# Graph attention on one core: one-hots turned by a compare instead of a transpose, and queries spread in fp32

## The chip, the cores and the metric

The kernel runs on one core of a Trainium2 chip. The metric is the device time of one execution in microseconds. TensorE (PE) multiplies matrices, VectorE (DVE) and ScalarE (ACT) do elementwise work, GpSimd (POOL) issues the gathers, SyncE (SP) issues most other DMAs.

## The reference, cut to what matters

Four pairs of a graph layer and a mixture of experts run one after the other over 3125 nodes with 256 features and 53125 edges, each on the normalized x and added to x. Only the first pair is touched: attention over the edges that end in a node, with 8 heads and the edges' 8 attributes as bias, and then a small mixture of four experts. Up to the order of the additions, the attention is

```python
q, k, v = ln(x) @ Wq.T, ln(x) @ Wk.T, ln(x) @ Wv.T      # 8 heads of 32
logit[e] = scale * (q[dst[e]] * k[src[e]]).sum(-1) + edge_attr_8[e]
a = softmax of logit over the edges with the same dst
x = x + (segment_sum(a * v[src], dst)) @ Wo.T
x = x + experts0(ln(x))      # shared MLP of three layers + 4 experts, the best two weighted
```

The graph, expert and attention layers that follow are the same in both kernels.

## The kernel before, in words

The edges are sorted by destination. The 3125 destinations form T = 25 tiles of P = 125. Each tile has a window of WC = 18 chunks of 128 edges that holds all edges ending in it; edges of a neighbouring tile in that window give one-hot rows of zeros.

**Setup** (lines 1640 to 1787) loads x group by group, normalizes it, writes keys and values to DRAM (kv_d, 2 KB a node in fp32) and the normalized rows, transposed, to lt_d. It fetches the windows' source and destination indices and attributes with indirect DMAs (90 partitions of 128 edges, five times), transposes them so that an edge lies on a partition (turned, L1730), and keeps src_w and row_w (the destination within its tile, bf16). The pools of the setup are then closed.

**The loop** (L1915 to L1950) takes the tiles in three phases at once: now (logits), before (the tile ahead of it: weights, sum, output), after (the next: its one-hots and queries). For one tile these are

- gathered (L1655): 6 indirect DMAs for 6 chunks of keys and values into one of 7 buffers kv, three buffers a tile.
- one_hot (L1797): oh, edges on partitions, 128 x 18 x 126 in bf16, by one comparison (one_hots, L282); also the loads of lt_t (L1804) and eb_t (L1806).
- one_hot_turned (L1821): oht, destinations on partitions: 18 transposes on PE (L1826) and three copies from PSUM on ACT (L1827).
- queries (L1809): q of the tile by one fp32 product of two terms, scaled by ACT (L1815) and split in three bf16 parts whose sum is q: DVE L1816, DVE L1817, ACT L1818, DVE L1819.
- logits (L1831): for every chunk, three bf16 products of oht with the parts of q (L1840) give each edge its query in PSUM (qx, two buffers of two chunks). DVE multiplies the keys with it (L1843) and adds up by head (L1844).
- sums_of (L1848): bias, exponential, sum by destination with oh (L1856).
- weights_of (L1860): the sums' logarithm back at the edges with oht (L1868), subtraction, exponential (L1873).
- weighted (L1875): DVE multiplies the values with the weights (L1878, once for 6 chunks), ACT turns oh into fp32 (oh_f, L1883), PE sums the rows of each destination in fp32 (acc, L1885, 18 products of 265 columns).
- normed, normed_turned, projected (L1889 to L1909): division, transposition, product with Wo, addition to x. normed also keeps deg, the number of a node's edges (L1890).

Between these, beside() runs a step of the experts (Experts0, L793) for two finished tiles at a time: normalize, transposed (L245), gates, and nine hidden products whose bias and ReLU relu_into (L776) gives in turn to DVE (L779) and ACT (L781). Windows prepares indices for the stage after the loop, blocks(), which counts edges between tiles.

The order of the work on each engine is not that of the source: a scheduler that knows the dependences lays the instructions of all engines out, and each engine runs its own list in order. Pools set which buffer an instruction waits for.

```python
pool = tiles          # 2 buffers of each name, opened ahead of the setup
psum = ...            # name="sm" 3 banks, "qx" 2, "acc" 1
```

Of the kernel before, what the change touches and what calls it, by code (L numbers as in the profile page):

```python
# [70 lines left out]
def gnn_ffn_kernel(ctx: ExitStack, tc: tile.TileContext, a, out: bass.AP):  # L71
# [173 lines left out]
    def transposed(psum, dst, src, n, relu=False):  # L245

        for k in range(2):
            ps = psum.tile([128, 512], F32, name="tr")
            for i in range(n):
                nc.tensor.transpose(ps[:, i * P:(i + 1) * P], src[:, i, k * 128:(k + 1) * 128],  # L250
                                    ident[:P, :P])
            of = ps[:, :n * P].rearrange("f (i p) -> f i p", i=n)
            if not relu:
                evacuate(dst[:, k, :n, :], of)
# [518 lines left out]
            evacuate(wt[:ne, :n, :].rearrange("e i p -> e (i p)"), ps[:ne, :n * P])  # L773
            return wt

    def relu_into(dst, ps, bias):  # L776
# [16 lines left out]
    class Experts0:  # L793


        def __init__(self, pools):
            pool = pools.enter_context(tc.tile_pool(name="ex0_b", bufs=1, side="right", reuse_waits="tile"))
            psum = pools.enter_context(tc.tile_pool(name="ps_ex0_b", bufs=1, space=PSUM, side="right",
                                                    reuse_waits="tile"))
            wpool = pools.enter_context(tc.tile_pool(name="w0", bufs=1, side="right", reuse_waits="tile"))  # L800
            with weights_of_pool(wpool, (SLOT0, D)):
                self.group = experts0_by(pool, psum, 2)
            self.now, self.left = iter(()), [(t0, min(2, T - t0)) for t0 in range(0, T, 2)]

        def step(self, ready):
# [5 lines left out]
                return self.step(ready)  # L811
            return False

    def experts0_by(pool, psum, most):

        wp = Packer()
        sw1 = wp.put(kk(a["sW1"]), 128, (2, 256))
# [28 lines left out]
        def group(t0, n):  # L846
# [4 lines left out]
            transposed(psum, lt, ln, n)  # L851
            yield
            g = gates(pool, psum, lt, n, gw, gb, 4, "softmax", ahead)
            yield
# [3 lines left out]
            def hidden(name, m, terms, bias):  # L858
                ps = tr()
                product(ps[:m, :c], terms)  # L860
                relu_into(name, ps[:m, :c], bias)
# [11 lines left out]
            for p in range(2):  # L873
                ps2 = psum.tile([128, 512], F32, name="pair", bufs=1)
                for j in range(2):
                    e = 2 * p + j
                    e1 = pool.tile([128, most * P], F32, name="e1")
                    hidden(e1[:, :c], 128, [(ew1[:, e, k, :], fan(lt[:, k, :n, :])) for k in range(2)],
                           cols[:, 3 + e:4 + e])
                    yield  # L880
                    product(ps2[j * 64:(j + 1) * 64, :c], [(ew2[:, e, :], e1[:, :c])])
                relu_into(e2[:, p, :c], ps2[:, :c], cols2[:, p:p + 1])
# [744 lines left out]
    def attention(windows, experts):  # L1627
# [5 lines left out]
        lt_d = dram.tile([2, 128, T, P], F32, name="lt_d")  # L1633
        eb_d = dram.tile([128, T, H, WC], F32, name="eb_d")
        win_d = dram.tile([T * WC], I32, name="win_d")
        KO, VO, AO = 16, 16 + D, 7
        WB = T * WC // 5
        with ExitStack() as es:
# [96 lines left out]
            def edges_in():  # L1735
# [51 lines left out]
            setup.close()  # L1787


            pool = tiles  # L1790
            psum = es.enter_context(tc.tile_pool(name="ps_att", bufs=3, space=PSUM, reuse_waits="tile"))
            windows.begin(first, lambda: psum.tile([128, 512], F32, name="sm"))

            class Tile:
                pass

            def one_hot(t):  # L1797
                s = Tile()
                s.t, s.kv = t, begun if t == 0 else []
                oh = pool.tile([128, WC, HC], BF16, name="oh")  # L1800
                one_hots(oh, row_h[:, t * WC:(t + 1) * WC, :], iota_h)
                s.oh = oh[:, :, :P]
# [4 lines left out]
                return s  # L1807

            def queries(s):  # L1809
# [8 lines left out]
                nc.scalar.copy(s.q[:, 1, :], q)  # L1818
                nc.vector.tensor_sub(s.q[:, 2, :], q, s.q[:, 1, :])  # L1819

            def one_hot_turned(s):  # L1821
                s.oht = pool.tile([P, WC, 128], BF16, name="oht")
                for c0 in range(0, WC, PC):
                    ps = psum.tile([128, 1024], BF16, name="sm")
                    for c in range(PC):
                        nc.tensor.transpose(ps[:P, c * 128:(c + 1) * 128], s.oh[:, c0 + c, :], ident_h)  # L1826
                    nc.scalar.copy(s.oht[:, c0:c0 + PC, :].rearrange("d c e -> d (c e)"),  # L1827
                                   ps[:P, :PC * 128])
                s.l = pool.tile([128, WC, H], F32, name="l")

            def logits(s, p):  # L1831

                if p == len(s.kv):
                    s.kv.append(gathered(s.t * WC + p * PC))
                kv = s.kv[p]
                for c0 in range(0, PC, 2):
                    ps = psum.tile([128, 2, D], F32, name="qx", bufs=2)
                    for c in range(2):
                        for k in range(3):
                            nc.tensor.matmul(ps[:, c, :], s.oht[:, p * PC + c0 + c, :], s.q[:, k, :],  # L1840
                                             start=(k == 0), stop=(k == 2))
                    k_ = kv[:, c0:c0 + 2, KO:VO]
                    nc.vector.tensor_mul(k_, k_, ps)  # L1843
                nc.vector.tensor_reduce(  # L1844
                    s.l[:, p * PC:(p + 1) * PC, :],
                    kv[:, :, KO:VO].rearrange("p c (h d) -> p c h d", h=H), AX.X, ALU.add)
# [40 lines left out]


            def normed(s):  # L1889
                nc.vector.tensor_copy(deg[:, s.t:s.t + 1], s.acc[:, H:H + 1])  # L1890
                inv = pool.tile([P, H], F32, name="inv")
                nc.vector.tensor_scalar(inv, s.acc[:, 0:H], 1.0e-30, None, ALU.max)
                nc.vector.reciprocal(inv, inv)
                s.ao = pool.tile([P, D], F32, name="ao")
# [4 lines left out]
            def normed_turned(s):  # L1899
                ps = psum.tile([128, 2, P], F32, name="sm")  # L1900
                for k in range(2):
                    nc.tensor.transpose(ps[:, k, :], s.ao[:, k * 128:(k + 1) * 128], ident[:P, :P])
                s.at = pool.tile([128, 2, P], F32, name="at")
                nc.scalar.copy(s.at, ps)

            def projected(s):
# [4 lines left out]
            now, before = one_hot(0), None  # L1911
            one_hot_turned(now)
            queries(now)
            more = experts()
            for t in range(T + 1):  # L1915
                def beside():
                    more.step(t - 1)

                if now:
                    logits(now, 0)  # L1920
                beside()
# [2 lines left out]
                    beside()  # L1924
                    weighted(before)
                beside()
                after = one_hot(t + 1) if t + 1 < T else None
                if before:
                    normed(before)
                if after:  # L1930
# [588 lines left out]
```

## Time and profile before

| What | Value |
|---|---|
| median of 3 runs | 3410.41 us (3407.14 to 3412.61) |
| the profiled execution, its own time | 3415.6 us |
| its span in the profile | 3413.8 us |
| busy PE, DVE, ACT, POOL | 3132.9, 1742.2, 1034.0, 680.0 us |
| attention loop, PE's first turned one-hot to the start of the next stage | about 113 to 925 us |
| start of acc (L1885), first tile and last | 150.9 and 906.2 us |
| mean clock of PE that the throttle granted | 0.951 |

The profile is one execution. A row of a group of instructions has the line, the engine, the operation, the tiles written and read, the shape and the count; then busy us and mean ns of one; then the engine's idle time just before them and what ended it. PE's rows overlap[...]; so the distance of their starts, not their length, is what one costs in a stream. A row of the timeline has the start, the length, the engine, the line and how many instructions were merged in it. PE's weight loads (PEld) run beside its matmuls.

### The profile page before, as it was taken

The numbers are of one execution on the slowest core, as the hardware profiler recorded it, in microseconds if no ns is written. First come the engines' busy times: TensorE is split into PE (matmuls) and PEld (weight loads), VectorE is DVE, ScalarE is ACT, GpSimd is POOL, SyncE is SP. The second block draws the span as 40 slices with busy tenths as digits, with TensorE's granted clock in tenths as the row PEclk, the third lists the DMA queues.
The fourth block names the chain that finished last, engine by engine and source line by source line (L and its number), as shares of the span: only waits on it lengthen the run. The fifth ranks groups of instructions, "written<-read, shape, count | busy, mean of one in ns | idle before, by whom it ended". The sixth has DMA issues, their size and how long they took to land. (4 is left out here: it accounts for less than half of the span.)

```text
span 3413.8 us, 45380 instructions
## 1 busy us (share of the span) xinstructions
PE 3132.9 (92%) x16587; PEld 2446.2 (72%) x16587; DVE 1742.2 (51%) x4905; ACT 1034.0 (30%) x1996; POOL 680.0 (20%) x639
## 2 busy tenths in 40 slices
PE   6688998998888899999996999979999999999898
PEld 2466776777677789898885888868755555579666
DVE  6577778777697534344674122155521111355662
ACT  1222332332255423232331222234423232332120
POOL 1665564655100000000134333200000000000000
PEclk9789998999889999999997999989999999999997
DMA  5755554555256734444344666553200000043001
GB/s 165 235 172 150 160 163 143 160 165 144 61 165 215 192 99 119 102 108 110 91 123 133 185 178 180 167 137 103 69 19 10 10 19 10 7 122 100 21 1 39
DMA packets 253208, 388.23 MB, mean 114 GB/s; under 512 B 41454, under 2 KB 201069, under 8 KB 252973
## 3 DMA queue, kind: packets, MB, share of 16 engines
q1 hardware_dynamic: 184090, 226.68, 23.3%
q0 software_dynamic: 54064, 141.25, 15.3%
q10 hardware_dynamic: 14819, 17.27, 1.9%
q8 instruction: 134, 2.20, 0.3%
q14 instruction: 101, 0.83, 0.1%
HBM read 314.47 MB, written 70.58 MB: 113 GB/s over the span
## 5 line engine op out<-in xcount | busy, mean ns | idle before, releaser
L2222 PE MATMUL agg<-cnt_f,hp 125*128 125x500 f32 (+1 forms) x3500 | 733.1, 369 | 22.2 <-ACT hp L2163 22.0
L2222 PEld LDWEIGHTS agg<-cnt_f,hp 125*128 125x128 f32 x3500 | 635.5, 189 | 103.2 <-ACT hp L2163 23.1
L1660 POOL DMA_INDIRECT kv<-kv_d,src_w x450 | 450.9, 1002 | 281.5 <-PE acc L1885 140.5
L2200 ACT CAST cnt_f<-blk 125x500 fp32r<-125x500 bf16 (+1 forms) x435 | 245.5, 565 | 518.4 <-PE agg L2222 496.7
L2200 DVE CAST cnt_f<-blk 125x500 fp32r<-125x500 bf16 (+1 forms) x440 | 185.5, 423 | 265.5 <-PE agg L2222 221.6
L1382 DVE SCALAR_TENSOR_TENSOR x<-po,gall,x 125x256 f32<-125x256 f32 x200 | 93.8, 484 | 417.5 <-PE po L266 416.9
L1376 ACT ACTIVATE h<-hid_ps,shift,scale 128x500 f32<-128x500 f32 (+1 forms) x224 | 161.9, 723 | 376.0 <-PE hid_ps L266 375.5
L1840 PE MATMUL qx<-q_t,oht 125*128 125x256 bf16 x1350 | 216.2, 296 | 53.9 <-DVE kv L1843 41.2
L1885 PE MATMUL acc<-kv,oh_f 128*125 128x265 f32 x900 | 224.9, 412 | 14.6 <-DVE kv L1878 14.6
L1885 PEld LDWEIGHTS acc<-kv,oh_f 128*125 128x125 f32 x900 | 178.5, 201 | 54.2 <-DVE kv L1878 18.5
L1840 PEld LDWEIGHTS <-oht 125*128 125x128 bf16 x1350 | 138.2, 105 | 100.4 <-issue 50.6
L266 PE MATMUL po<-wslot,h 128*125 128x256 f32 x800 | 203.0, 386 | 0.1
L266 PEld LDWEIGHTS po<-wslot,h 128*125 128x125 f32 x800 | 145.0, 187 | 75.2 <-ACT h L1376 27.0
L266 PE MATMUL hid_ps<-h,wslot 128*128 128x500 f32 (+1 forms) x448 | 193.8, 556 | 4.1 <-ACT h L1376 0.6
L266 PE MATMUL hid_ps<-xe,wslot 128*128 128x256 f32 x832 | 187.3, 383 | 1.8 <-DVE xe L1214 1.8
L1072 POOL DMA_INDIRECT xs_d<-r_l,pos x50 | 60.2, 1204 | 645.3 <-DVE r_l L1068 567.1
L266 PE MATMUL hid_ps<-v_rows,wslot 128*128 128x500 f32 (+1 forms) x448 | 186.8, 537 | 0.0
L1225 ACT ACTIVATE hid<-hid_ps,wslot 128x256 f32<-128x256 f32 x208 | 98.5, 475 | 286.8 <-PE hid_ps L266 286.8
L266 PE MATMUL po<-wslot,hid 128*128 128x256 f32 x832 | 184.5, 378 | 0.0
L266 PEld LDWEIGHTS hid_ps<-xe,wslot 128*128 128x128 f32 x832 | 150.7, 191 | 33.4 <-ACT hid L1225 4.1
L266 PEld LDWEIGHTS po<-wslot,hid 128*128 128x128 f32 x832 | 155.7, 189 | 21.8
L1843 DVE TENSOR_TENSOR kv<-kv,qx 128x512 f32<-128x512 f32 x225 | 150.7, 679 | 26.2 <-PE qx L1840 24.7
(512 smaller groups left out, 4625.8 us busy)
## 6 DMA issues: line engine op xcount, KB each, us to landing
wslot<-in_ex_W SPq DMA_DIRECT2D x52, 1024.0 KB
blk<-an_d SPq DMA_DIRECT2D x60, 546.9 KB
blk<-at_d SPq DMA_DIRECT2D x40, 546.9 KB
blk<-an_d SPq DMA_DIRECT2D x45, 410.2 KB
at_d<-ab SPq DMA_DIRECT2D x25, 683.6 KB
an_d<-an SPq DMA_DIRECT2D x25, 683.6 KB
blk<-at_d SPq DMA_DIRECT2D x30, 410.2 KB
kv<-kv_d,src_w POOLq DMA_INDIRECT x450, 3.7
```

The source lines that it names most:

```text
L266: nc.tensor.matmul(ps, l, r, start=(bias is None and i == 0), stop=(i == last))
L1072: st = nc.gpsimd.indirect_dma_start(out=xs_d, in_=l2[:, i, :].bitcast(I32), in_offset=None, out_offset=bass.IndirectOffsetOnAxis(ap=self.p ...
L1225: nc.scalar.activation(hid[:, m, :], ps[:, :BLK], AF.Gelu, bias=c[:, 4 + m:5 + m])
L1376: nc.scalar.activation(dst[:, m, :c], ps[:, :c], AF.Relu, bias=shift[:, l, col:col + 1], scale=scale[:, l, col:col + 1])
L1382: nc.vector.scalar_tensor_tensor(x[:, t0 + i, :], po, gating.all[:, t0 + i, e:e + 1], x[:, t0 + i, :], ALU.mult, ALU.add)
L1660: got = nc.gpsimd.indirect_dma_start(out=kv[:, c, KO:], out_offset=None, in_=kv_d, in_offset=bass.IndirectOffsetOnAxis(ap=src_i[:, at + c: ...
L1840: nc.tensor.matmul(ps[:, c, :], s.oht[:, p * PC + c0 + c, :], s.q[:, k, :], start=(k == 0), stop=(k == 2))
L1843: nc.vector.tensor_mul(k_, k_, ps)
L1885: nc.tensor.matmul(s.acc[:, :D + H + 1], of[:, c, :], kv[:, c, AO:VO], start=(p == 0 and c == 0), stop=(p == 2 and c == PC - 1))
L2200: to(f[:, :n, :], part[0][:, :n, m % MB, :])
L2222: nc.tensor.matmul(ps[f][:, :c], hp[:, m, k, f * 128:(f + 1) * 128], got[:, :c], start=(m == 0 and k == 0), stop=(m == T - 1 and k == 1))
```

## The change

- **one_hot_turned** no longer transposes. In the setup, the destinations within the tile are also written, in bf16, to a new tensor turned_d in DRAM, 450 chunks of 128 edges. asked(t), at the head of a loop pass, loads the 18 chunks of a tile to all 125 partitions (576 KB), with lt_t and eb_t. DVE compares the loaded rows in place with the partition's number; ACT makes three fp32 copies oht_f of 6 chunks each, in three buffers.
- **queries** ends with ACT's scaling; q stays in fp32. **logits** takes one fp32 product a chunk in place of three bf16 ones.
- **The experts beside the loop** have all their ReLUs and both copies of transposed on ACT. normed copies deg on ACT.
- The loop's tiles lie in a pool of their own, opened after the setup is closed; ao and at have one buffer instead of two.

```diff
@@ relu_into (experts0_by and Experts0 pass on_act=True; transposed gets to=nc.scalar.copy) @@
-        if turn[0]:
+        if turn[0] and not on_act:
             nc.vector.tensor_scalar(dst, ps, bias, 0.0, ALU.add, ALU.max)
         else:
             nc.scalar.activation(dst, ps, AF.Relu, bias=bias)
@@ attention, setup @@
+        turned_d = dram.tile([T * WC, 128], BF16, name="turned_d")
...
+            first_row = pool.tile([WB, 1], F32, name="first_row", bufs=1)
+            nc.vector.memset(first_row, 0.0)
+            for k in range(1, 5):
+                nc.vector.scalar_tensor_tensor(first_row, pcol[:WB], k * WC - 0.5, first_row, ALU.is_gt, ALU.add)
+            nc.vector.tensor_scalar(first_row, first_row, float(P), None, ALU.mult)
...
                         nc.vector.tensor_copy(wf, w)
+                        if to is dst_f:
+                            wr = pool.tile([WB, 128], BF16, name="wr")
+                            nc.vector.tensor_scalar(wr, wf, first_row, float(b * 5 * P), ALU.subtract, ALU.subtract)
+                            nc.sync.dma_start(turned_d[b * WB:(b + 1) * WB, :], wr)
@@ attention, loop @@
-            pool = tiles
+            pool = es.enter_context(tc.tile_pool(name="att_s", bufs=2, reuse_waits="tile"))
...
-            def one_hot(t):
+            def asked(t):
...
+                s.oht = pool.tile([P, WC, 128], BF16, name="oht")
+                move(nc.sync, s.oht.rearrange("d c e -> d (c e)"), turned_d[t * WC:(t + 1) * WC, :].rearrange("(o c) e -> o (c e)", o=1)
+                     .to_broadcast([P, WC * 128]))
                 s.lt = pool.tile([128, 2, P], F32, name="lt_t")
...
-                s.q = pool.tile([P, 3, D], BF16, name="q_t")
-                q = pool.tile([P, D], F32, name="q")
-                nc.scalar.activation(q, ps, AF.Copy, scale=float(HD) ** 0.5)
-                nc.vector.tensor_copy(s.q[:, 0, :], q)
-                nc.vector.tensor_sub(q, q, s.q[:, 0, :])
-                nc.scalar.copy(s.q[:, 1, :], q)
-                nc.vector.tensor_sub(s.q[:, 2, :], q, s.q[:, 1, :])
+                s.q = pool.tile([P, D], F32, name="q")
+                nc.scalar.activation(s.q, ps, AF.Copy, scale=float(HD) ** 0.5)
 
             def one_hot_turned(s):
-                s.oht = pool.tile([P, WC, 128], BF16, name="oht")
+                v = s.oht.rearrange("d c e -> d (c e)")
+                nc.vector.tensor_scalar(v, v, pcol[:P], None, ALU.is_equal)
+                s.oht_f = []
                 for c0 in range(0, WC, PC):
-                    ps = psum.tile([128, 1024], BF16, name="sm")
-                    for c in range(PC):
-                        nc.tensor.transpose(ps[:P, c * 128:(c + 1) * 128], s.oh[:, c0 + c, :], ident_h)
-                    nc.scalar.copy(s.oht[:, c0:c0 + PC, :].rearrange("d c e -> d (c e)"),
-                                   ps[:P, :PC * 128])
+                    s.oht_f.append(pool.tile([P, PC, 128], F32, name="oht_f", bufs=3))
+                    nc.scalar.copy(s.oht_f[-1], s.oht[:, c0:c0 + PC, :])
...
                     for c in range(2):
-                        for k in range(3):
-                            nc.tensor.matmul(ps[:, c, :], s.oht[:, p * PC + c0 + c, :], s.q[:, k, :],
-                                             start=(k == 0), stop=(k == 2))
+                        nc.tensor.matmul(ps[:, c, :], s.oht_f[p][:, c0 + c, :], s.q, start=True, stop=True)
...
-                nc.vector.tensor_copy(deg[:, s.t:s.t + 1], s.acc[:, H:H + 1])
+                nc.scalar.copy(deg[:, s.t:s.t + 1], s.acc[:, H:H + 1])
```

The loop calls asked(t + 1) ahead of logits, one_hot(after) where one_hot(t + 1) stood, and one_hot_turned(after) after it as before.

More of the change, by code (lines that the diff above doesn't have):

```diff
@@ L243, in normalize, with transposed @@
                                     ALU.subtract, ALU.mult)
-    def transposed(psum, dst, src, n, relu=False):
+    def transposed(psum, dst, src, n, relu=False, to=None):
         for k in range(2):
@@ L253, in transposed @@
             if not relu:
-                evacuate(dst[:, k, :n, :], of)
+                (to or evacuate)(dst[:, k, :n, :], of)
             elif k:
@@ L774, in __call__, with relu_into @@
             return wt
-    def relu_into(dst, ps, bias):
+    def relu_into(dst, ps, bias, on_act=False):
         turn[0] ^= 1
-        if turn[0]:
+        if turn[0] and not on_act:
             nc.vector.tensor_scalar(dst, ps, bias, 0.0, ALU.add, ALU.max)
@@ L801, in __init__ @@
             with weights_of_pool(wpool, (SLOT0, D)):
-                self.group = experts0_by(pool, psum, 2)
+                self.group = experts0_by(pool, psum, 2, True)
             self.now, self.left = iter(()), [(t0, min(2, T - t0)) for t0 in range(0, T, 2)]
@@ L812, in step, with experts0_by @@
             return False
-    def experts0_by(pool, psum, most):
+    def experts0_by(pool, psum, most, on_act=False):
         wp = Packer()
@@ L850, in group @@
             lt = pool.tile([128, 2, most, P], F32, name="lt")
-            transposed(psum, lt, ln, n)
+            transposed(psum, lt, ln, n, to=nc.scalar.copy if on_act else None)
             yield
@@ L860, in hidden @@
                 product(ps[:m, :c], terms)
-                relu_into(name, ps[:m, :c], bias)
+                relu_into(name, ps[:m, :c], bias, on_act)
             s1 = pool.tile([128, 2, most * P], F32, name="s1")
@@ L881, in group @@
                     product(ps2[j * 64:(j + 1) * 64, :c], [(ew2[:, e, :], e1[:, :c])])
-                relu_into(e2[:, p, :c], ps2[:, :c], cols2[:, p:p + 1])
+                relu_into(e2[:, p, :c], ps2[:, :c], cols2[:, p:p + 1], on_act)
                 ps = tr()
@@ L1795, in attention @@
                 pass
-            def one_hot(t):
+            def asked(t):
                 s = Tile()
                 s.t, s.kv = t, begun if t == 0 else []
-                oh = pool.tile([128, WC, HC], BF16, name="oh")
-                one_hots(oh, row_h[:, t * WC:(t + 1) * WC, :], iota_h)
-                s.oh = oh[:, :, :P]
+                s.oht = pool.tile([P, WC, 128], BF16, name="oht")
+                move(nc.sync, s.oht.rearrange("d c e -> d (c e)"), turned_d[t * WC:(t + 1) * WC, :].rearrange("(o c) e -> o (c e)", o=1)
+                     .to_broadcast([P, WC * 128]))
                 s.lt = pool.tile([128, 2, P], F32, name="lt_t")
@@ L1807, in one_hot @@
                 return s
+            def one_hot(s):
+                oh = pool.tile([128, WC, HC], BF16, name="oh")
+                one_hots(oh, row_h[:, s.t * WC:(s.t + 1) * WC, :], iota_h)
+                s.oh = oh[:, :, :P]
             def queries(s):
@@ L1893, in normed @@
                 nc.vector.reciprocal(inv, inv)
-                s.ao = pool.tile([P, D], F32, name="ao")
+                s.ao = pool.tile([P, D], F32, name="ao", bufs=1)
                 nc.vector.tensor_mul(s.ao.rearrange("p (h d) -> p h d", h=H),
@@ L1902, in normed_turned @@
                     nc.tensor.transpose(ps[:, k, :], s.ao[:, k * 128:(k + 1) * 128], ident[:P, :P])
-                s.at = pool.tile([128, 2, P], F32, name="at")
+                s.at = pool.tile([128, 2, P], F32, name="at", bufs=1)
                 nc.scalar.copy(s.at, ps)
@@ L1909, in projected @@
                 nc.vector.tensor_add(x[:, s.t, :], x[:, s.t, :], po)
-            now, before = one_hot(0), None
+            now, before = asked(0), None
+            one_hot(now)
             one_hot_turned(now)
@@ L1917, in beside @@
                     more.step(t - 1)
+                after = asked(t + 1) if t + 1 < T else None
                 if now:
@@ L1926, in attention @@
                 beside()
-                after = one_hot(t + 1) if t + 1 < T else None
+                if after:
+                    one_hot(after)
                 if before:
```

## The prediction

> **What bounds the kernel now.** I read the page's busy totals and lines first, then the busy time by stretches, then the waits and the timeline inside the attention loop, the only place that the change touches at length. The page's chain of waits is no help here: it names none of the loop's lines among its shares. The loop runs from about 113 us (first turned one-hots) to 925 us, 25 tiles of destinations, so 812 of 3413.8 us. The two stretches below are 23 tiles of it, and two tiles in which TensorE had its full clock.
>
> ```profile
> 150.90:877.90 727.00, 656.07 (x4303) 510.44 (x4304) 565.16 (x1222) 208.94 (x418) 430.29 (x421) 0.93 0.55 157
> ...
> 431.20:494.10 62.90, 55.48 (x385) 43.28 (x385) 48.98 (x105) 18.52 (x37) 40.83 (x37) 1.00 0.53 153
> ```
>
> The columns are the length, then busy us of PE, PE's weight loads, DVE, ACT and POOL, the clock, DMA share and GB/s. PE is busy 90% and DVE 78%; ACT has 71% free. A tile takes 31.6 us at clock 0.93 and 31.5 at 1.00, so PE's rate alone doesn't set the time: the two queues wait for each other in fixed orders. How much PE really works is read from the spacing of its rows:
>
> ```profile
> 443.19 1.03 PE L266 MATMUL sm<-wq,lt_t 128*125 128x256 f32 x4
> 444.06 0.59 PE L266 MATMUL tr<-wslot,s 128*125 128x256 f32 x2
> ...
> 450.94 1.47 PE L1840 MATMUL qx<-q_t,oht 125*128 125x256 bf16 x12
> 454.03 0.71 PE L1840 MATMUL qx<-q_t,oht 125*128 125x256 bf16 x5 [1.62 <-DVE kv L1843]
> ```
> ```profile
> 604.00 1.21 PE L1826 MATMUL sm<-ident_h,oh 128*125 128x128 bf16 x18
> 605.05 0.38 PE L770 MATMUL tr<-ident,g 125*4 125x125 f32 x2
> ```
>
> Four fp32 rows of 256 columns take 444.06-443.19, **0.217 us a row**, and queries() issues only two fp32 products there: each fp32 product is two rows, so 0.43 us. Twelve bf16 rows span 1.47 less the last one's 0.27: **0.109 us a row**. Eighteen transposes take 1.05, **0.058 us each**. At such spacings, every kind counted, PE has some 24.7 us of work a tile, and 31.6-24.7, about 7 us, is waiting or a slowed clock. Part of the waiting is this (waits in the 727 us; total us, times, longest):
>
> ```profile
> PE qx L1840 <- DVE kv L1843: 28.7, 23, 1.8
> ...
> PE acc L1885 <- DVE kv L1878: 12.2, 20, 2.7
> ...
> PE qx L1840 <- DVE q_t L1819: 5.7, 9, 0.6
> ...
> PE qx L1840 <- ACT q_t L1818: 5.5, 3, 1.9
> ```
>
> The first is PE waiting for one of two qx buffers, which DVE's product with the keys (L1843) frees. The last two are the end of queries(): ACT, DVE, DVE, ACT, DVE split q in three bf16 parts, and PE waits for the last. DVE's price per six chunks is in these lines of the page and of its timeline:
>
> ```profile
> L1843 DVE TENSOR_TENSOR kv<-kv,qx 128x512 f32<-128x512 f32 x225 | 150.7, 679 | 26.2 <-PE qx L1840 24.7
> ```
> ```profile
> 451.64 1.75 DVE L1844 TENSOR_REDUCE l<-kv 128x48 f32<-128x1536 f32 x1
> ```
>
> Three times 0.68 and one 1.75 are 3.8 us; PE needs 18 x 0.109, 1.96 us, for the same chunks. DVE can't keep up while PE does nothing but qx.
>
> [...] The one-hot of before (L282, tensor_tensor, 2268 elements) takes 1.34 us[...]; no tensor_scalar of this shape is in the trace.
>
> **The change part by part.**
>
> *PE.* Out: 1350 bf16 rows of L1840 x 0.109 = 147 us, and 450 transposes of L1826 x 0.058 = 26 us. In: 450 fp32 products of 256 columns, two rows each, 900 x 0.217 = 195 us. **PE's work grows by 22 us**, 0.9 a tile; fp32 weight loads of 0.19 us stay under rows of 0.217, as at L266 now. On the slowed share of the loop it is somewhat more: +23.
>
> *DVE.* Out: 25 x (0.34+0.42+0.42) of L1816, L1817, L1819, 29 us; 65 ReLUs of the experts (L779, 60 of the full width) at 0.47, 30 us; 13 copies of lt (L224) at 0.415, 5 us; 25 copies of deg, 4 us: 68 us. In: 25 compares of 2304 bf16 elements with a column. [...] Setup adds some 10 short instructions, about 2 us, beside PE's. **DVE's work falls by about 49 us** (2 a tile)[...].
>
> *ACT.* Out: 75 copies of turned one-hots (0.80) and 25 casts of q (0.405), 70 us. In: 75 casts to fp32 of 768 elements, nearest row L1883's 0.82 for 750, 62 us; 65 ReLUs at 0.47, 30; 13 lt copies at 0.37, 5; 25 deg copies at some 0.2, 5. Net +32 on 229 us: covered by 71% idle, except that a ReLU can now stand behind an instruction of ACT's that waits, such as deg's for the end of acc (L1885). In the built order the ReLUs that PE needs soonest stand ahead of it; I allow nothing, with 0 to +10 for the range.
>
> *SP and the DMAs.* Five writes of 23 KB in setup, and for each tile two loads of together 576 KB, one row for all 125 partitions, before lt_t and eb_t in SP's queue. The load waits until the older tile's weights_of is done with the buffer (PE at L1868), and DVE compares after that same tile's three products L1878. Between lie 6.4 us (147.84 to the end of L1878 at 154.2) to 10. Nearest transfers: at_d's 684 KB write ended 3.1 to 4.1 us after its issue, lt_t's small load 2.3 to 3.7 with the gathers beside it. Estimate 4 to 6 us: covered. lt_t of a tile is ordered a whole tile ahead, so queueing behind this load costs nothing. The kv gathers (18 x 4 KB x 128 a tile) lose under a tenth of the DMA engines to it; DVE waits for a gather almost never now.
>
> *Start of the loop.* The new pool lies over the setup's, so the first load comes after the setup's last transposes and after five eb_d writes, the last issued at 114.5; landing at about 119[...]. The second stands behind the experts' weights in SP's queue (last at 129.9): qx of tile 1 some 2 us late. **+3 us**, between 0 and +8.
>
> *Waits that go.* (a) L1840's wait for L1843: six chunks now take PE 2.6 us instead of 1.96 plus 0.35 of transposes elsewhere, DVE still 3.8: the shortfall in an unbroken stretch falls from 1.85 to 1.2, 35%, and DVE comes to it earlier. Of the 32 us that the loop has of it (41.2 in the page, less 9.6 at its start) I take 18. (b) The q chain is one ACT copy, far ahead of its use in the built order: 11 us. (c) PE waits for turned one-hots' copies: 2. (d) DVE does 2 us a tile less ahead of L1878, lt and the rest that PE waits for; of some 30 us of such waits I take 12. Sum -43, between -15 and -70.
>
> Against the profiled execution's 3415.6: +23 +3 -43 = -17, 3399. The median of the runs stood 5.2 under that execution: **3393**. The end of the loop and all later stages keep their instructions; blocks() may see one group of the experts with its ReLUs on ACT, nothing.
>
> **Rivals.** *DVE sets the pace*: then its whole relief counts, -49 +3, 3364. For it: clock 0.93 costs no time against 1.00. Against: ReLUs and q chain lie partly in DVE's idle time. *PE's longer work is exposed*: DVE's relief falls where PE isn't waiting, and only q's 11 us go: 3410 +23 +3 -11 = 3425. It decides when less than 26 us of waits vanish; PE's 90% speaks for it. *The load is late*: if the same row read 125 times lands later than 7 to 10 us after its issue, DVE stands at the compare with everything behind it, and ACT's cast and oh_f behind that; at 10 us some 2 us a tile, +50: about 3443. *The gain doesn't come out*: fewer waits just pay for the longer rows, 3410.
>
> **How the numbers follow.** Main case (3375 to 3403) 0.50; DVE's pace 0.15; even 0.14; PE exposed 0.15; late load 0.06. About 0.2%, 6.8 us, is what a measurement of this kernel can tell from no change: faster 0.65, same 0.14, slower 0.21. The range 3360 to 3428 leaves out the late load and the tail of DVE's pace.
>
> **What would show it.** Right: L1849's fp32 rows 900 at 0.217 apart;[...] PE's waits for L1851 (old L1843) under 20 us; a tile of about 30.8 us; compare never waiting for oht. Wrong: DVE waits on DMA oht,[...] PE waits for ACT's ReLUs, or stages after 925 us that differ.

## The result, and the profile after

| | before | after |
|---|---|---|
| median of 4 runs each | 3411.51 us (3407.14 to 3413.11) | 3376.61 us (3369.13 to 3376.88) |
| ratio | 1 | 0.9894, 95% interval 0.9877 to 0.9912 |
| the profiled execution, its span | 3413.8 us | 3374.6 us |
| first product of qx starts | 119.7 us | 124.3 us |
| from there to the start of the last tile's acc | 786.6 us | 741.5 us |
| from there to the first agg of the next stage | 243.9 us | 243.7 us |
| the rest | 2263.6 us | 2265.0 us |

The change took 35 us off, 1.06% by the ratio above (0.88 to 1.23%). The whole gain is made in the attention loop: 4.7 us are lost ahead of it, 45 won in it, 1 lost behind it. The stretch of the changed kernel that answers to the 727 us shown of the kernel before (length, busy us of PE, PE's weight loads, DVE, ACT, POOL, then clock, DMA share, GB/s):

```profile
149.00:876.00 727.00, 677.28 (x3678) 537.48 (x3678) 557.03 (x1148) 246.07 (x508) 442.69 (x422) 0.96 0.63 176
```

More of PE's time is busy (677 of 727 us where it was 656), and the clock is 0.96 where it was 0.93. PE does more work in the loop and finishes it sooner. Over the whole loop, from the first qx to the last acc, the two kernels stand so, before and then after:

```profile
119.60:906.20 786.60, 697.48 (x4585) 541.86 (x4583) 605.31 (x1301) 221.17 (x443) 451.50 (x442) 0.93 0.54 155
```
```profile
124.30:865.90 741.60, 686.68 (x3719) 543.81 (x3719) 570.04 (x1149) 248.89 (x509) 458.48 (x439) 0.96 0.65 181
```

The lines of the page for the spreading of q, before and then after, and for the multiplication with the keys after. Their last figures are the idle time of the engine ahead of them and what ended most of it:

```profile
L1840 PE MATMUL qx<-q_t,oht 125*128 125x256 bf16 x1350 | 216.2, 296 | 53.9 <-DVE kv L1843 41.2
```
```profile
L1849 PE MATMUL qx<-q,oht_f 125*128 125x256 f32 x900 | 240.3, 399 | 14.6 <-DVE kv L1851 11.6
...
L1851 DVE TENSOR_TENSOR kv<-kv,qx 128x512 f32<-128x512 f32 x225 | 150.7, 680 | 32.6 <-PE qx L1849 29.9
```

The wait of PE for the qx buffers was 41.2 us in the page of the kernel before and is 11.6. It is DVE now that waits more for PE (29.9 us, 24.7 before). The waits in the loop of the changed kernel (total us, times, longest):

```profile
DVE kv L1667 <- PE acc L1893: 37.6, 21, 4.5
...
DVE oht L1834 <- DMA oht<-turned_d: 23.2, 10, 7.1
...
PE sm L1864 <- ACT el L1861: 12.2, 13, 2.7
...
PE qx L1849 <- DVE kv L1851: 11.6, 16, 3.3
...
PE tr L266 <- DVE kv L1667: 10.7, 3, 6.2
...
PE tr L250 <- DVE ln L242: 6.3, 8, 1.3
```

The first two are new waits of DVE. L1667 sets the column of ones in a fresh kv buffer, for which the acc of an older tile must be done; L1834 is the compare, and it does wait for its rows. The four of PE are what is left or new there: the exponential ahead of the sums, the qx buffers, DVE standing at L1667, the experts' normalization. The timeline shows one of the late loads, and what a row of the new product costs:

```profile
448.47 0.82 DVE L1834 TENSOR_SCALAR oht<-oht,pcol 125x2304 bf16<-125x2304 bf16 x1 [4.35 <-DMA oht<-turned_d]
...
449.32 1.56 ACT L1838 CAST oht_f<-oht 125x768 f32<-125x768 bf16 x2 [4.71 <-DVE oht L1834]
...
466.11 0.60 PE L1849 MATMUL qx<-q,oht_f 125*128 125x256 f32 x2
...
466.54 1.01 PE L266 MATMUL tr<-s,wslot 128*128 128x250 f32 x4
...
467.39 1.03 PE L1849 MATMUL qx<-q,oht_f 125*128 125x256 f32 x4
```

466.54-466.11 is 0.43 us for the two rows of one chunk. The compare takes 0.82, and ACT starts its copies right behind it.

**PE's time in three terms.** For every row of PE in the loop I took the distance to the next row. Up to the usual distance of its kind and shape (the 15th percentile over the run) it counts as work. What is beyond counts as a wait where PE stood idle for more than 30 ns ahead of the next row, and as slowed where it did not. The last column is not part of the sum: it is the time in the loop for which the clock record shows half speed.

| in the loop, us | length | work | waits | slowed | half clock |
|---|---|---|---|---|---|
| before | 786.6 | 600.7 | 114.2 | 71.7 | 117.6 |
| after | 741.5 | 622.9 | 68.8 | 49.9 | 55.5 |
| difference | -45.1 | **+22.2** | **-45.4** | **-21.8** | -62 |

Of the slowed time, 45.1 us before and 21.6 us after lie within the stretches at half clock, so the fall of that term is all there. In these stretches the rows of qx that follow one another without a gap start 0.213 us apart at L1840 of the kernel before, elsewhere 0.109; at L1849 of the changed kernel they start 0.427 us apart, elsewhere 0.216 (medians). The three terms are an account of where the time went; that one of them fell doesn't yet say why.

### The profile page after: what moved, and what is told of

It is laid out like the page before. It is cut to its first block, busy times and chain, and to the rows that moved or that the text cites. A ratio compares the mean times of both kernels' runs of the same rounds, so it can differ in the third digit from the quotient of the medians.

```text
span 3374.6 us, 43621 instructions
## 1 busy us (share of the span) xinstructions
PE 3116.4 (92%) x15687; PEld 2442.6 (72%) x15687; DVE 1704.7 (51%) x4763; ACT 1064.6 (32%) x2074; POOL 691.1 (20%) x639
## 4 chain that ended last, share of the span: by engine, by line
PE 67%; DVE 5%; DMA 3%; issue 3%; ACT 2%; POOL 0%; SPq 0%; ACTq 0%; POOLq 0%; DVEq 0%
PE agg L2233 21%; PE po L266 19%; PE hid_ps L266 15%; PE tr L266 2%; PE row L266 1%; PE tok L1536 1%; PE acc L1893 1%; PE tr L2321 1%; PE tr L250 1%; DVE hr L282 1%; DMA kv<-kv_d,src_w 1%; PE qx L1849 1%; ACT h L1376 1%; DVE hc L282 0%; PE s L266 0%
## 5 line engine op out<-in xcount | busy, mean ns | idle before, releaser
L1661 POOL DMA_INDIRECT kv<-kv_d,src_w x450 | 467.4, 1039 | 233.5 <-issue 109.5
L1849 PE MATMUL qx<-q,oht_f 125*128 125x256 f32 x900 | 240.3, 399 | 14.6 <-DVE kv L1851 11.6
L1849 PEld LDWEIGHTS qx<-q,oht_f 125*128 125x128 f32 x900 | 170.2, 197 | 50.3 <-DVE kv L1851 20.8
L266 PEld LDWEIGHTS po<-wslot,hid 128*128 128x128 f32 x832 | 155.7, 189 | 21.8
L1851 DVE TENSOR_TENSOR kv<-kv,qx 128x512 f32<-128x512 f32 x225 | 150.7, 680 | 32.6 <-PE qx L1849 29.9
## 6 DMA issues: line engine op xcount, KB each, us to landing
oht<-turned_d SPq DMA_DIRECT2D x25, 504.0 KB
```

The source lines that it names most:

```text
L266: nc.tensor.matmul(ps, l, r, start=(bias is None and i == 0), stop=(i == last))
L1661: got = nc.gpsimd.indirect_dma_start(out=kv[:, c, KO:], out_offset=None, in_=kv_d, in_offset=bass.IndirectOffsetOnAxis(ap=src_i[:, at + c: ...
L1849: nc.tensor.matmul(ps[:, c, :], s.oht_f[p][:, c0 + c, :], s.q, start=True, stop=True)
```

## The experiments

Theory A: PE waited for DVE because DVE can't keep up while PE runs qx (3.8 us for six chunks, PE 1.96) and because q goes through a chain of five steps; the fp32 product is slower (0.43 us a chunk, where three bf16 rows take 0.33) and needs no split, so both waits go. Theory A also supposes that the half clock goes with such waits; from before to after it fell from 117.6 to 55.5 us. Rival B: the gain is DVE's relief by the ReLUs and copies moved to ACT. Rival C: the gain is the 450 transposes that PE no longer does. The parts can be built one by one. They ran in three sets, each with the kernel before on the same chip. **The second set's chip ran the kernel before in 3412.08 us, as the prediction's did. The first and the third set came to chips on which it took 3792.51 and 3772.34 us**; their loops stand still in a way that the loop on the second set's chip does not, and they have a part of their own below. All three parts that hold the compare or the fp32 product also keep the changed kernel's pool, its order of loads and its single buffers of ao and at, so what these do is not told apart from the parts.

### The compare alone

```diff
 # of the change, kept: turned_d, its load, the compare; back as before:
-                        nc.tensor.matmul(ps[:, c, :], s.oht_f[p][:, c0 + c, :], s.q, start=True, stop=True)
+                        for k in range(3):
+                            nc.tensor.matmul(ps[:, c, :], s.oht[:, p * PC + c0 + c, :], s.q[:, k, :],
+                                             start=(k == 0), stop=(k == 2))
 # and the split of q, no oht_f, ReLUs and copies in turn
```

> Compare from DRAM rows, bf16 products of the split q, ReLUs and copies as before, once more. Where the kernel before takes some 3411 us: theory A 3405 to 3418 (PE comes 26 us sooner to qx buffers that DVE hasn't freed, DVE has 20 us more); rival B +10 to +20; rival C 3380 to 3390.

Measured 3412.51 us, ratio 0.9998 (0.9986 to 1.0010): no difference. Of C's 22 to 30 us nothing is left in the whole. A's number held; its reason held only in part. PE's work in the loop fell by 25.0 us (600.7 to 575.7; the step of the prediction had 26). The loop fell by 13.4 of them, and 8.1 of these were lost ahead of it, where qx began later since the first rows have to come from DRAM (their load was issued at 115.1 and 115.6 us in two halves, their compare began at 123.5); 2.7 more went behind the loop. Inside the loop 12.3 us came back as waits (114.2 to 126.5), and the half clock stayed (117.6 to 114.4). But the wait that A had named, for the qx buffers, did not grow: on the page it fell from 41.2 us, of which 9.6 were one wait in the first tile, to 19.0:

```profile
L1851 PE MATMUL qx<-q_t,oht 125*128 125x256 bf16 x1350 | 206.9, 296 | 25.5 <-DVE kv L1854 19.0
```

In its place PE waits longer ahead of the sums for ACT's exponential (22.3 us of the waits, 1.9 before), for a ReLU of the experts on DVE (10.6) and for DVE's division of the output (9.3). So it is the loop as a whole that takes half of the transposes' time back, not the pair of qx buffers.

### The fp32 product alone

```diff
 # transposes and copies to oht as before; then
+                    s.oht_f.append(pool.tile([P, PC, 128], F32, name="oht_f", bufs=3))
+                    nc.scalar.copy(s.oht_f[-1], s.oht[:, c0:c0 + PC, :])
 # q in fp32, one product a chunk, ReLUs and copies in turn
```

> q in fp32 with one fp32 product a chunk, transposes and their copies as before, once more. Where the kernel before takes some 3411 us: theory A 3395 to 3415 (48 us more of PE's work, 30 to 40 less of waits, 15 to 25 less of half clock); rival B 3401 to 3411; rival C 3445 to 3458.

Measured 3405.08 us, ratio 0.9982 (0.9975 to 0.9989): some 6 us faster, with 46.5 us more work on PE (600.7 to 647.2). (The profiled execution, from which the terms come, took 3400.74.) C had +35 to +48 and is out again. The waits fell by 42.2 us (114.2 to 72.0) and half-clock time from 117.6 to 57.4 us. The wait for the qx buffers is all but gone: 4 us of the waits, 51 before. A new one stands in its place (waits, total us, times, longest):

```profile
PE qx L1840 <- ACT q L1817: 22.9, 13, 2.0
```

The timeline of this kernel shows why. PE has ended the product with Wq some 1.1 us after its start; ACT, with six copies to make where the kernel before and the changed kernel have three, comes to q 1.8 us later:

```profile
457.46 1.13 PE L266 MATMUL sm<-wq,lt_t 128*125 128x256 f32 x4 [0.19 <-ACT oht L1827]
...
458.00 0.84 ACT L1829 CAST oht_f<-oht 125x768 f32<-125x768 bf16 x1
...
458.84 0.83 ACT L1829 CAST oht_f<-oht 125x768 f32<-125x768 bf16 x1
459.56 0.81 ACT L1827 COPY oht<-sm 125x768 bf16<-125x768 bf16 x1
460.25 0.22 ACT L740 ACTIVATE g<-g 125x8 f32<-125x8 f32 x1
460.36 0.39 ACT L1817 ACTIVATE q<-sm 125x256 f32<-125x256 f32 x1
460.63 0.84 ACT L1829 CAST oht_f<-oht 125x768 f32<-125x768 bf16 x1
...
460.81 0.96 PE L1840 MATMUL qx<-q,oht_f 125*128 125x256 f32 x2 [1.99 <-ACT q L1817]
```

### Both, without the part of ACT

```diff
 # the changed kernel with on_act=False, transposed and deg as before:
-                self.group = experts0_by(pool, psum, 2, True)
+                self.group = experts0_by(pool, psum, 2)
-                nc.scalar.copy(deg[:, s.t:s.t + 1], s.acc[:, H:H + 1])
+                nc.vector.tensor_copy(deg[:, s.t:s.t + 1], s.acc[:, H:H + 1])
```

> The changed kernel with the experts' ReLUs and the copies of lt and deg where they were, once more, since in the first set the loop of the kernel before took 1091 us for 24 tiles where it takes 755 in the run that the prediction read. Where the kernel before takes some 3411 us: theory A (PE waits less for DVE because the fp32 product is slower and q needs no split) 3380 to 3390; rival B (the relief of DVE by ACT brings the gain) 3405 to 3412; rival C (the transposes' going) 3376 to 3382.

Measured 3384.98 us, ratio 0.9932 (0.9912 to 0.9952), 27 us faster: A's number. B, the relief of DVE, is out for three quarters of the gain. The terms of these three and of the two kernels before and after:

| in the loop, us | first qx | length | work | waits | slowed | half clock |
|---|---|---|---|---|---|---|
| before | 119.7 | 786.6 | 600.7 | 114.2 | 71.7 | 117.6 |
| compare alone | 127.8 | 773.2 | 575.7 | 126.5 | 71.0 | 114.4 |
| fp32 product alone | 112.8 | 777.5 | 647.2 | 72.0 | 58.3 | 57.4 |
| both | 123.7 | 745.5 | 622.3 | 69.9 | 53.3 | 56.0 |
| both and ACT (after) | 124.3 | 741.5 | 622.9 | 68.8 | 49.9 | 55.5 |

The work adds up: -25.0 and +46.5 make +21.5, and both have +21.6. The waits don't: +12.3 and -42.2 would make -29.9, and both have -44.3. Of the 14 us more, the wait for q may be the larger share: it takes 25.0 us of the waits of the fp32 product alone, and less than 1 us with the compare, where ACT has no copies from PSUM to make ahead of q. That these copies are the cause is read from the timeline above; no run tests it by itself. What the runs do show is that **the parts pay together**: the step from transposes to the compare shortens the loop by 13.4 us with three bf16 products and by 32.0 us (777.5 to 745.5) with the fp32 product, for the same 25.0 us of PE's work. Some of it is lost again ahead of the loop, where qx begins 8.1 and 10.8 us later.

The part of ACT is the step from 3384.98 to 3376.61 us. The two intervals (0.9912 to 0.9952, 0.9877 to 0.9912) just meet, so some 8 us are likely and not certain. In the traces 4.0 us of it lie in the loop and 4.7 between the last acc and the next stage, where the last experts run.

### The column of ones on GpSimd

```diff
-                nc.vector.memset(kv[:, :, KO - 1:KO], 1.0)
+                nc.gpsimd.memset(kv[:, :, KO - 1:KO], 1.0)
```

> The changed kernel with kv's column of ones set by GpSimd in its own queue of gathers in place of DVE. In the changed kernel's trace DVE stood 37.6 us at this memset for the end of acc, and PE waited 11.1 us for DVE behind it. If those waits are exposed: 3360 to 3370, against 3376.6 of the changed kernel. If DVE then stands at the compare or at the gather instead: within 4 us of 3376.6. If 75 memsets slow the row of gathers: 3380 or more. Where the kernel before takes 3792 us, as in the first set, it stands for the whole change: theory A has it near no_act's 3693.

Measured 3379.18 us, ratio to the kernel before 0.9910 (0.9892 to 0.9929): by the two ratios no different from the changed kernel, which was not run on this chip itself. DVE's 37.6 us at L1667 and PE's 11 behind it are gone, but PE's waits as a whole only fell from 68.8 to 65.9 us; a new 9.5 of them are for DVE's L885 of the experts. qx began 2.3 us later. The wait that was taken away was largely replaced by others.

### The other chips

The first set had the three parts of above and the part of ACT alone (only the ReLUs and the copies of lt and deg on ACT, all else as before).

> The kernel before with the experts' ReLUs, the copies of lt and deg on ACT; transposes and three bf16 products stay. Theory A (the gain of the whole change is PE waiting less for DVE because the fp32 product is slower and q needs no split; half-clock time falls with those waits): DVE loses 39 us of work, but its shortfall in an unbroken stretch of qx chunks stays, so only waits for lt, L1878 and the like shrink: 3400 to 3408, -3 to -10 us. Rival B (the loop's gain is DVE's relief by the ReLUs and copies): 3375 to 3388, -25 us or more. Rival C (the gain is the transposes' going): no change, 3408 to 3414.

> The changed kernel with the experts' ReLUs and the copies of lt and deg where they were (compare and fp32 product stay). Theory A: most of the gain stays, 3380 to 3390, -22 to -30 us against the kernel before. Rival B (the relief by ACT): 3405 to 3412. Rival C (the transposes' going): 3376 to 3382, all of it stays.

> The kernel before with the turned one-hots compared from DRAM rows; three bf16 products of the split q, ReLUs and copies as before. PE loses 26 us of transposes, DVE gains 20 us of compares. Theory A: PE comes sooner to the qx buffers that DVE hasn't freed, so its wait for them grows by about what the transposes took: 3405 to 3418, -5 to +8. Rival B: slower, +10 to +20, since DVE only gets more to do. Rival C: 3380 to 3390, -22 to -30.

> The kernel before with q kept in fp32 and one fp32 product a chunk; the 450 transposes and their bf16 copies stay, ACT makes the fp32 copies besides. PE has 48 us more work than before, DVE 29 us less (no split of q). Theory A: the waits for the qx buffers and for q fall by 30 to 40 us and the half-clock time by some 15 to 25, so the sum is -15 to +5: 3395 to 3415. Rival B: 0 to -10. Rival C (PE's work is what counts): +35 to +48, 3445 to 3458.

| chip of 3792.51 us | us | ratio (95%) | loop | waits | half clock |
|---|---|---|---|---|---|
| part of ACT alone | 3793.40 | 1.0002 (0.9990 to 1.0014) | 1119.7 | 372.0 | 440 |
| fp32 product alone | 3784.32 | 0.9973 (0.9963 to 0.9984) | 1126.2 | 325.2 | 437 |
| compare alone | 3700.75 | 0.9769 (0.9746 to 0.9791) | 1058.7 | 357.8 | 410 |
| both | 3693.15 | 0.9747 (0.9726 to 0.9769) | 1053.4 | 317.4 | 333 |

None of the absolute times expected can be held against these. As differences, A had the part of ACT alone at -3 to -10 us, the compare alone at -5 to +8 and both at -22 to -30; they came to +1, -92 and -99. Only the fp32 product alone, -8, lies where A had it (-15 to +5). The order is another: here the compare brings nearly all. The stages behind the loop take what they took on the chip of the prediction (from the last acc to the end 2504 us for the part of ACT alone, 2508 for the kernel before). What differs is the loop, and in the kernels without the compare also what lies ahead of it: qx begins at 155.8 us in the part of ACT alone and at 144.0 in the fp32 product alone, where the latter began at 112.8 in the second set. The kernel before was not traced on these chips. The timeline of the part of ACT alone shows the standstills:

```profile
654.22 1.03 PE L266 MATMUL sm<-wq,lt_t 128*125 128x256 f32 x4
...
655.30 0.49 PE L1840 MATMUL qx<-q_t,oht 125*128 125x256 bf16 x3
655.73 0.95 POOL L1660 DMA_INDIRECT kv<-kv_d,src_w  x1 [0.30 <-issue]
656.99 0.95 POOL L1660 DMA_INDIRECT kv<-kv_d,src_w  x1 [0.30 <-issue]
658.24 0.95 POOL L1660 DMA_INDIRECT kv<-kv_d,src_w  x1 [0.30 <-issue]
659.49 0.95 POOL L1660 DMA_INDIRECT kv<-kv_d,src_w  x1 [0.30 <-issue]
660.20 0.38 SPq L1804 DMA_DIRECT2D lt_t<-lt_d  x1
660.21 0.38 ACT L1815 ACTIVATE q<-sm 125x256 f32<-125x256 f32 x1 [5.01 <-remote]
```

The product with Wq runs from 654.22 to some 655.3. Both that wait for it, ACT's q and SP's next load of lt_t, go only at 660.2, and from 655.8 on nothing but POOL's gathers runs. Over the 24 tiles between the first and the last acc of that kernel (1091 us), PE, DVE and ACT all stand at once for 189 us. In all but 2 of these packets of gathers move (to within half a microsecond), though they move in only 52% of the stretch; in the kernel before on the chip of the prediction, all three stand at once for 1 us. Whether the gathers hold the other engines back no run tests, and why the compare helps there no run tells either; the part of ACT alone was not run on a chip like the prediction's, nor the changed kernel on these.

The third set was built for the loop as it is on the second set's chip and came to a chip of 3772.34 us. Two kernels leave out the sum over each head's 32 products (1.75 us of DVE for six chunks), meant to let DVE keep up:

```diff
-                nc.vector.tensor_reduce(
-                    s.l[:, p * PC:(p + 1) * PC, :],
-                    kv[:, :, KO:VO].rearrange("p c (h d) -> p c h d", h=H), AX.X, ALU.add)
+                nc.vector.tensor_copy(s.l[:, p * PC:(p + 1) * PC, :], kv[:, :, KO:KO + H])
```

> The kernel before without the sum over each head's 32 products: L1844's reduction of 1536 elements (1.75 us, 75 times) becomes a copy of 48 of them, so DVE has some 120 us less and keeps up with PE. The logits are then single products. Theory A (in the kernel before, PE's waits for DVE and the half-clock time behind them cost what PE's shorter work saves): PE's waits fall from 99 us to 35 to 50 and the slowed rest from 69 to 25 to 40, the 24 tiles from 755 to 650-680 us, the whole 3310 to 3340. Rival D (the fp32 product is faster of itself, whatever DVE does): the 24 tiles stay over 710 us, 3370 or more.

> The changed kernel with the same reduction left out. Theory A: PE's 19 us of longer work now show, since there is little left to wait for: the 24 tiles take 650 to 680 us and 0 to 25 us more than in the kernel before without the reduction; 3310 to 3350, no faster than that one. Rival D: the changed kernel keeps its 35 us of lead, -25 us or more against the kernel before without the reduction.

Measured 3767.88 us (0.9988, 0.9980 to 0.9997) and 3689.74 us (0.9778, 0.9762 to 0.9795). The whole times are no measure here: on other values the stages behind the loop take 34 and 44 us longer (2298 and 2307 us from the first agg to the end, 2264 in the kernel before). The loops take 1068.6 and 1013.2 us, so the changed kernel keeps a lead of 55. But PE still waits for 352 and 268 us of them, where A had 35 to 50 left: without DVE's sums this chip's loop still has its standstills (205 and 192 us), so the pair can't tell A from D. A's numbers missed, D's lead stands only for this chip, and what the fp32 product does where DVE keeps up is left open for the loop as it is in the second set.

```diff
 # load_twice: move(nc.sync, s.oht..., turned_d[...]) is issued two times in asked
 # sums_later: sums_of(now) behind logits(now, 2) becomes
 #             sums_of(before) behind logits(now, 0)
```

> The changed kernel with every tile's load of the edges' rows issued twice into the same buffer, so DVE's compare gets it later. In the changed kernel DVE stood 24 us at the compare for it, PE 2 us for what comes of it. If the load is hidden with room to spare: within 4 us of the changed kernel's 3376.6. If it is at the edge of being hidden: +10 to +40, with DVE's wait for the load at 60 us or more and PE waiting for the fp32 copy of it.

> The changed kernel with the sums of a tile's exponentials written down after the next tile's first six chunks instead of ahead of them, since PE's longest wait left is 15 us for ACT's exponential there. If that wait is exposed and goes: 3362 to 3372 against 3376.6. If PE then waits at the weights' product for the sums instead (DVE's L1866 and L1872 come later): within 4 us, or up to 10 slower.

Measured 3660.08 us (0.9706, 0.9689 to 0.9722) and 3684.84 us (0.9769, 0.9741 to 0.9797). There is no run of the changed kernel on this chip to hold them against. Beside each other: with every load issued twice DVE waited 18.2 us for the rows where the other waited 2.6, and the kernel was 25 us faster all the same; the cause of the 25 us is not known. Neither question is answered: how near the load is to being exposed, and whether later sums pay, stay open.

## Why the prediction was right, and where it was not

It was right in the sign, the place and most of the mechanism; the time was 16 us below the forecast of 3393, inside the range and at the lower edge of the main case. The gain was twice the forecast: the sum was -17 against the profiled execution, and -39 came out. A tile between the first acc and the last took 29.7 us (712.8 for 24), where 30.8 were forecast and the kernel before had 31.5.

- **PE +22, +23 on the slowed clock.** +22.2. The compare alone measured the bf16 side and the transposes (-25.0), the fp32 product alone the other (+46.5). Two rows of 0.217 for one fp32 product was the right price: the rows of L1849 start 0.216 us apart (median at full clock).
- **Start +3.** +4.7; inside 0 to +8.
- **Waits -43.** -45.4, but not of the parts it was made of; that the total fits is luck, since (a) was 18 us too small and (d) 19 too large. (a) The wait for the qx buffers was put at -18 and was -36 (50.6 to 14.4 us of the waits above). About 10 of the 50.6 were one wait in the first tile, which the forecast had set aside. For the rest I took the shortfall of an unbroken stretch, while in the timeline at 466 us the products of qx stand between others of the experts, which give DVE more of the time it needs; and the compare alone had already brought this wait from 50.6 to 30.1 with the bf16 products, which the forecast had not seen. (b) q's chain, -11: -13. (c) The copies of turned one-hots, -2: -3. (d) DVE's relief, -12: the other waits together rose by 7. L1878's wait did fall, 17.9 to 2.6, but it was 5.2 without ACT's part already; the exponential ahead of the sums (1.9 to 15.1), the column of ones (1.5 to 11.1) and the experts' L242 (0 to 7.9) came up in its place. The prediction had said that the queues wait for each other in fixed orders, but its sum gave no place to what would be late next. (a) to (d) add up to -45.
- **The clock: the step that failed.** The sum had only a +1 for more work on the slowed share and no term for the share itself. The slowed term fell by 21.8 us, and this is the whole difference between -17 and -39. The half-clock time of the loop fell from 117.6 us in 21 intervals to 55.5 in 10 and the end of one that had begun ahead of the loop. I had read that two tiles at clock 1.00 were as long as the mean, and concluded that the clock costs nothing. Two tiles were too few for that: rows of L1840 start 0.213 us apart at half clock and 0.109 elsewhere, and over the ten middle pairs of tiles of the kernel before, a pair is on average 0.36 us longer for each us of half clock in it (correlation 0.7), and the waits in it don't grow with the half clock; pairs that begin one tile later give 0.18 (correlation 0.7). For the 62 us less of half clock that makes an estimate of 11 to 22 us. What brings the half clock no run shows. The kernel before has its two qx buffers, after the first tile no stop of PE over 2.7 us, and half clock for 103.8 of the 755.3 us from the first acc to the last. In the five kernels of the table of parts the half clock goes with the product (114 to 118 us with bf16 rows, 56 to 57 with fp32 rows), and with it the number of PE's stops (145 and 154 with bf16 rows, 75 to 87 with fp32 rows) and the waits as a whole (114 and 127 us, 69 to 72). It does not go with the stops of over 1 us: the fp32 product alone has 23 of them, the kernel before 25. Whether the fewer stops, the longer rows or something else keep the clock up, these runs don't separate; on the chips of the first set the fp32 product alone left the half clock where it was (437 us, 440 in the part of ACT alone).
- **DVE -49.** The forecast left 19 us for the 25 compares, the author's estimate, with nothing in the trace of before behind it. They took 0.814 us each (median; 0.802 to 0.899), 20.5 us in all. 67.9 us of DVE's work went, 20.5 and 1.9 of setup came: -45.5.
- **ACT +32, covered.** 62.2 for the copies, 30 for the ReLUs, +30.6 busy on the page. PE waits for a ReLU on ACT 0.7 us in the whole loop.
- **The load is covered.** The compare waited for its rows 11 times, 24.1 us in all and up to 7.1, where the prediction had "never" and listed such waits among the signs of being wrong. In those it went 5.4 to 9.2 us after the issue of the load, so 4 to 6 us to land was too short. Little of it reaches PE directly: PE waits for oht_f 0.5 us in the whole loop. What the rest of DVE's queue lost behind it was not measured. The rival of the late load (+50) is out. In the 727 us the queue with the load took 8.8% of the DMA engines' time, 2.2% before; the queue with the gathers took 54.0%, 52.4% before, and moved 109.5 MB, 108.9 before: some 4.7 MB a tile, half of what the prediction counted.
- **Later stages nothing.** -0.2 and +1.4 us. But the part of ACT moved 4.7 us there, against the kernel with both other parts.

Of the rivals, "PE exposed" needed waits of less than 26 us to go; 45 went. "DVE sets the pace" had 3364: its time was nearer than the main case's, but its reason fits neither the ones on GpSimd nor the part of ACT, each of which takes a wait or work from DVE and brings 0 to 8 us.

## What to carry to other kernels

PE waited for DVE on two qx buffers here (41.2 us on the page of the kernel before), and a longer instruction cost less there than its work: with 46.5 us more of work in it, the loop came out 9 us shorter. So price such an instruction by what is left after the waits it fills. And a part that only shortens the waiting engine's work may bring little until the waits are gone: the 25.0 us of the transposes were worth 13 us of the loop without the fp32 product and 32 with it. Build the parts one by one and together, and look in each at what stands ahead of the result that is waited for: with six copies to make, ACT came to q 1.8 us after PE had ended its product. Give the clock a term of its own in the sum whenever stops of PE go: here half-clock time fell by half (114 to 118 us, 56 to 57) in the kernels in which the number of stops did (145 and 154, 75 to 87).

## What the runs showed that was not expected

- Half clock came in a loop where PE is busy 89% (697.5 of 786.6 us) and, after the first tile, stood still for no more than 2.7 us at a time: 117.6 us of it. After the change it was 55.5 of 741.5. Every piece that begins in the loop is one to four times 3.4 us.
- The same kernel took 3410, 3412, 3772 and 3792 us on the chips it came to. In the kernels that were traced on the slow ones, the loop with the indirect gathers was longer, and without the compare the start ahead of it too. There PE, DVE and ACT stood together for 160 to 205 us of the loop, all but 3 us of that within half a microsecond of a moving packet of the gathers; on the others for 0 to 5 us. Which parts of a change pay was another question there: the compare alone brought 2.3%, and nothing in the second set.
- A row of 2304 bf16 elements sent to all 125 partitions (562.5 KB in two loads, 504.0 and 58.5) landed 5.4 to 9.2 us after its issue where DVE had to wait for it, and within 6.4 to 9.8 us where it had not.
